# Cross-attention and FFN: the Gate's tokens turned in the attention stage, in 32x32 blocks on VectorE and by plain DMAs, in place of transposing DMAs

## The chip, the cores and the metric

The kernel runs on one core of a Trainium2 chip. The core has five engines, each with an instruction stream of its own: PE (TensorE: matmuls, and transposes as matmuls with an identity), DVE (VectorE), ACT (ScalarE), POOL (GpSimd) and SP (SyncE, which only issues DMAs). 16 DMA engines move data between HBM and SBUF, the on-chip memory of 128 partitions; PE writes PSUM. An engine works through its stream in order: an instruction that waits holds all that stand behind it. The metric is the device time of one execution in microseconds, the median of several runs.

## The reference

```
x:   [16, 512, 512] f32      16 elements of 512 tokens with 512 features
ctx: [16, 120, 512] f32
x1 = x + attention(layernorm(x), ctx)          16 heads of 32, RoPE on queries and keys
t  = act_qdq(layernorm(x1))                    16-bit quantization, one scale for the whole tensor
up   = act_qdq(t @ w_up.T)                     weights quantized to 4 bits in blocks of 32
gate = act_qdq(t @ w_gate.T)                   1536 hidden features
gate = act_qdq(gate * sigmoid16(gate))
out  = x1 + act_qdq(gate * up) @ w_down.T
act_qdq(v): s = max|v| / 32767;  clip(round(v / s)) * s
```

The scale of `act_qdq` is taken over all 16 elements. So no token can be quantized for the FFN until the last element's attention is done, and the normalized tokens must be kept or made again in between.

## The kernel before

**Layout.** Tokens come with tokens on the partitions: an element is four tiles of 128 tokens by 512 features (index q). The FFN's matmuls need them turned: features on the partitions, 4 chunks (index d) of 128 features, by 512 tokens.

**Stages.** Attention (about the first 940 us of the trace), Gate (to about 1495), Up with the sigmoid and the product of gate and up (to about 2050), Down (to the end). In attention and in all three others the order on PE, DVE and ACT is written out by hand (`manual_schedule`), from Gate on POOL's too. What is left to SP, and in attention to POOL, is ordered by the framework's scheduler from its own estimates. The framework also gives the DMAs eight completion semaphores in turn, whatever queue issues them: a DMA is issued only when the one eight places before it has landed.

**Attention.** The loop runs over elements b, and inside it over four rounds g (groups of four heads). In a round PE makes the scores (L338), DVE reduces them to maxima (L344, L349), PE turns the maxima (`tm`, L356), DVE prepares them (L358 to L365), PE subtracts them (L373), ACT takes the exponential (L381), and PE forms values and sums (L389, L394). Between these stand the parts of the other elements: the queries of the next one (L317, L226 to L230), the reciprocals (L405, round 0), divisions (L418, round 1) and outputs (L424, L430, rounds 2 and 3) of the one before (`old`), the normalization of the element two ahead (`new`: statistics L112 on DVE in round 2, `normalize` L303 on POOL, PE's turn `tp_x` L212 in round 3), and the weight preparation for the FFN (`weight`).

The element two behind (`older`) has its x1 = x + attention in `xt`. `end()` (L441) stores x1 to HBM (`x1_d`). `end_normalize(q)` (L446, POOL) makes the normalized tokens `xn`, and `largest(q)` (L454, DVE) reduces them to their largest magnitude in `max_x`; q = 0 in round 0, q = 1 to 3 in round 2. The normalized tokens are then dropped. The last two elements are finished behind the loop (L654 to L679), the last with its normalization on DVE.

**First tokens.** Element 0 alone is turned early: in the last element's four rounds, `first_tokens` (L542) loads its x1 again, normalizes it on POOL, turns it on PE (`transposed`, L207: four PE transposes into a PSUM bank and one ACT copy) and leaves it in two buffers of the pool `ahead` (tag "a", two buffers, each [128, 2, 512] f32). The same two buffers are used by later stages.

**Gate.** `over_all` and `scale_of` (L702, L720) form the scale from `max_x`. L915 quantizes element 0 from the two buffers, `high` and `low` (L758, L761, L768) split it in three pieces of fewer bits, which are the matmuls' operands (`xm`, `xl`, `xh`). PE then works through 96 chunks (element b, two blocks f of 128 hidden features), some 5.4 us each. For the elements after the first, `load(b)` (L901) fetches x1 to `x1t` (one buffer), `normalize` (L920, POOL) normalizes it again, `quantize` (L927) converts it to 16-bit integers on ACT (`xi`) and a transposing DMA (L934, on SP's queue) puts it into `xq` (one buffer). Weights are loaded by `wg.load` (L753), 256 KB each, into 13 buffers for each of three kinds.

Of the kernel before, what the change touches and what calls it, by code (L numbers as in the profile page):

```python
# [9 lines left out]
F32 = mybir.dt.float32  # L10
F32R = mybir.dt.float32r
I32 = mybir.dt.int32
I16 = mybir.dt.int16
# [8 lines left out]
P = 128  # L22
# [31 lines left out]
def tile_xattn_ffn(  # L54
# [42 lines left out]
    xn_d = [dram.tile([P, ND, S], I16, name=f"xn_{b}") for b in range(B)]  # L97

    wg_d, wu_d, wd_d = (dram.tile([P, NF, 3, D], F32, name=f"w{k}_d") for k in "gud")
    x1_d = [dram.tile([NQ, P, D], F32, name=f"x1_{b}") for b in range(B)]  # L100

    g_d = dram.tile([B, P, 2, NF, S // 2], F32, name="g_d")
# [85 lines left out]
    with ExitStack() as at:  # L188
# [95 lines left out]
        class Element:  # L284
# [167 lines left out]
            def largest(self, q):  # L452
                i = self.b * NQ + q
                nc.vector.tensor_reduce(  # L454
                    max_x[:, i : i + 1], self.xn.pop(q), AX.X, ALU.max,
                    apply_absolute_value=True,
                )

        keys = {0: Keys(0)}
        wv_sb = load_weight(wv, "wv_sb", p1)  # L460
# [76 lines left out]
            )  # L537


        first = [ahead.tile([P, 2, D], F32, tag="a", name=f"first_{i}") for i in range(2)]  # L540

        def first_tokens(q):  # L542
            t = first[q // 2][:, q % 2, :]
            nc.sync.dma_start(t, x1_d[0][q])
            nc.gpsimd.tensor_scalar(
                t, t, ln_mv[:, 0, q, 0:1], ln_rstd[:, 0, q : q + 1], ALU.subtract, ALU.mult
            )
            transposed(t, P, t.rearrange("p (d t) -> p d t", t=P), f"first_{q}")

        for q in range(NQ):
# [14 lines left out]
        for b in range(B):  # L568
# [8 lines left out]
            for g in range(NG):  # L577
                if g == 0:
                    here.attend()
                    if older:  # L580
                        for q in range(3):
                            older.end_normalize(q)
                here.scores(g, keys[b // BC].kT)

                rest = []
                if g < 3:
                    if nxt:
                        rest.append(nxt.query((0, 2, 3)[g]))
# [12 lines left out]

                if weight and g == 2:
                    weight.load()
                if weight and g == 3:
                    weight.quantize()
                if older and g == 0:
                    older.largest(0)
                    older.end_normalize(3)
                if older and g == 2:
                    for q in range(1, NQ):  # L610
                        older.largest(q)
                if new and g == 2:
                    for q in range(NQ):
                        new.stats(q)
                    for q in range(3):
                        new.normalize(q)
                if b == B - 1:
                    first_tokens(g)

                if g == 0:  # L620
                    if old:
                        old.reciprocals()
                    if nxt:
                        nxt.query(1)()
                if g == 1 and old:
                    for i in range(2):
                        old.divide(i)
                if g < 2 and kvs:
                    kvs.go_on(2)
                if g == 1 and old:  # L630
                    for i in range(2, NG):
                        old.divide(i)
                if g == 2 and old:
                    for q in range(2):
                        old.output(q)()
                if g == 3:
                    if new:
                        new.turn(0)
                        new.normalize(3)
                    if old:  # L640
                        old.output(3)()
                        old.end()
                        old.inverse()
                    if new:
                        new.turn(1)
                    if weight:
                        rest = weight.turn(0)
                    if new:
                        new.turn(2)
                        new.turn(3)  # L650
                    if weight:
                        rest()
# [11 lines left out]
        for q in range(NQ):  # L664
            old.end_normalize(q)
            old.largest(q)
        for g in range(NG):
            last.divide(g, halves[1])
        for q in range(NQ):
# [4 lines left out]
            if q > 0:  # L674
                last.end_normalize(q - 1, nc.vector)
                last.largest(q - 1)
        last.end()
        last.end_normalize(NQ - 1, nc.vector)
        last.largest(NQ - 1)  # L679

        idle = bank("idle_0")
        for _ in range(18):
# [131 lines left out]
    with ExitStack() as gu:  # L814
# [84 lines left out]
        xs = {0: Tokens(0, "g")}  # L899

        def load(b):  # L901
            xs[b] = Tokens(b, "g")
            xs[b].x1 = wp.tile([P, NQ, D], F32, tag="x1t", name=f"x1t_{b}", bufs=1)
            nc.sync.dma_start(xs[b].x1, x1_d[b].rearrange("q p d -> p q d"))

        wg.load(range(4), (0,))
        wg.load(range(4), (1, 2))
        wg.load(range(4, 8))
        load(1)
        s_x, r_x = scale_of(over_all([max_x], "x"), 1.0, "x")  # L910
        s_xw = small.tile([P, 1], F32, name="s_xw")

        xs[0].room()
        for i, t in enumerate(first):
            nc.vector.tensor_scalar(  # L915
                xs[0].q[:, 2 * i : 2 * i + 2], t.rearrange("p q (d t) -> p q d t", t=P),
                r_x, None, ALU.mult,
            )

        def normalize(b, qs):  # L920
            for q in qs:
                nc.gpsimd.tensor_scalar(
                    xs[b].x1[:, q, :], xs[b].x1[:, q, :],
                    ln_mv[:, b, q, 0:1], ln_rstd[:, b, q : q + 1], ALU.subtract, ALU.mult,
                )

        def quantize(b):  # L927

            xi = wp.tile([P, NQ * D], I16, tag="xi", name=f"xi_{b}")
            nc.scalar.activation(  # L930
                xi, xs[b].x1.rearrange("p q d -> p (q d)"), AF.Copy, scale=r_x
            )
            xs[b].room()
            nc.sync.dma_start_transpose(xs[b].q.rearrange("p q d t -> p (q d) t"), xi)  # L934


        def up_weight(o):
# [21 lines left out]
        for d in range(ND):  # L959
            xs[0].high(d, nc.vector if d < 2 else nc.gpsimd)  # L960
            xs[0].low(d)
        normalize(1, range(NQ))
        xs[0].keep()
        nc.vector.tensor_scalar(s_xw, s_x, WHOLE, None, ALU.mult)

# [44 lines left out]
        for b in range(B):  # L1010
            for f in range(N2):
# [14 lines left out]
                def after():  # L1026
# [20 lines left out]
                    if b + 2 < B:  # L1047
                        if b > 0 and f == 0:
                            load(b + 2)
                        if f in ((2, 3) if b else (3, 4)):  # L1050
                            normalize(b + 2, (0, 1) if f == (2 if b else 3) else (2, 3))
                    if b == B - 1:
                        wu.load((0,) if f == 0 else (2 * f - 1, 2 * f))

# [479 lines left out]
```

## Time and profile before

| | |
|---|---|
| runs | 2598.81, 2604.08, 2605.47 us; median 2604.08 |
| profiled execution | 2608.83 us, of it span 2607.0 us; granted TensorE clock 0.986 |
| busy in the span | PE 2512.7 us (96%), DVE 2083.6 (80%), POOL 1576.6 (60%), ACT 1155.9 (44%) |
| DMA | 500.49 MB in 268146 packets, 192 GB/s |
| PE in Gate | a matmul of 128x128 by 512 tokens each 389 ns |
| `normalize` (L922) | 60 on POOL, 2137 ns each |
| quantization (L930) | 15 on ACT, 1990 ns each |
| transposing DMAs (L934) | 15 on SP's queue, 5.0 us from issue to landing |
| `largest` (L454) | 64 on DVE, 675 ns each |

The span runs from the first to the last instruction of the profiled execution. A row such as `527.13 1.86 DVE L454 TENSOR_REDUCE max_x<-xn 128x1 f32<-128x512 f32 x3` in the timeline reads: start and length in us, engine, line, operation, what is written from what, shapes, and how many like ones are merged; in brackets, where there are any, the idle time of the engine ahead of it and what ended it. SPq and ACTq are DMA issues by those engines. DMA share is the mean busy share of the 16 DMA engines.

### The profile page before, as it was taken

The page shows a single profiled execution, that of the slowest core. Times are in us where ns is not written, and L with a number is a line of the kernel's source. Part 1 is how long each engine was busy: PE and PEld are TensorE (multiplying, and loading weights), DVE is VectorE, ACT ScalarE, POOL GpSimd, SP SyncE. Part 2 cuts the span into 40 slices and gives each one's busy share as a digit, 9 for nine tenths or more (in the row PEclk, how much of TensorE's full clock was granted, in tenths as well). Part 3 has the DMA queues.
Part 4 walks back from the last instruction along what each step waited for, and adds up shares of the span by engine and source line. Part 5 has one row for each costly group of instructions (what it writes and reads, how often), then busy time and mean ns, then how long its engine had stood idle before and what let it go on. Part 6 is the DMA issues. An engine that isn't in the chain of part 4 may idle for free. (4 is left out here: it accounts for less than half of the span.)

```text
span 2607.0 us, 30411 instructions
## 1 busy us (share of the span) xinstructions
PE 2512.7 (96%) x10732; PEld 1690.9 (65%) x10732; DVE 2083.6 (80%) x2836; ACT 1155.9 (44%) x1311; POOL 1576.6 (60%) x1011
## 2 busy tenths in 40 slices
PE   8899999999999889999999999999999699999999
PEld 4334344333433268888878888888887478788887
DVE  4668886887888667786887589999998688888886
ACT  1222232222222225545445378888877344444442
POOL 3466665655675165545555057777766477777775
PEclk9899999999999989999999999999999799999999
DMA  4011121111120086767766789999889777777774
GB/s 161 20 65 49 49 93 59 57 59 49 49 77 33 22 277 214 250 202 244 226 217 217 238 300 332 322 344 330 296 290 322 295 280 253 248 248 248 251 249 145
DMA packets 268146, 500.49 MB, mean 192 GB/s; under 512 B 47440, under 2 KB 66000, under 8 KB 267984
## 3 DMA queue, kind: packets, MB, share of 16 engines
q1 hardware_dynamic: 267296, 496.90, 55.6%
q8 instruction: 85, 1.39, 0.2%
q10 hardware_dynamic: 528, 1.05, 0.1%
q14 instruction: 77, 0.63, 0.1%
q0 software_dynamic: 160, 0.52, 0.1%
HBM read 263.00 MB, written 227.54 MB: 188 GB/s over the span
## 5 line engine op out<-in xcount | busy, mean ns | idle before, releaser
L758 POOL TENSOR_SCALAR oh_d<-oq_d 128x512 fp32r<-128x512 int16 x190 | 398.0, 2117 | 160.8 <-DVE oq_d L1320 134.1
L1106 POOL TENSOR_TENSOR po<-gt,t_wu 128x1024 f32<-128x1024 f32 x96 | 231.7, 2413 | 208.2 <-DVE gt L1083 149.6
L317 PE MATMUL qp<-xnT,wq_sb 128*128 128x512 f32 x512 | 239.2, 610 | 2.5 <-ACT cT L213 2.5
L398 ACT COPY ao<-pv 128x512 f32<-128x512 f32 x64 | 37.5, 586 | 452.2 <-PE pv L389 452.2
L424 PE MATMUL op<-wo_sb,ao 128*128 128x512 f32 x512 | 233.2, 604 | 0.2 <-DVE ao L418 0.2
L1337 PE MATMUL dn_d<-wd,om_d 128*128 128x512 f32 x768 | 196.7, 406 | 22.7 <-DVE om_d L768 13.4
L782 PE MATMUL mm_wg<-xl_g,wg 128*128 128x512 f32 x768 | 205.4, 389 | 0.0
L782 PE MATMUL mm_wg<-xh_g,wg 128*128 128x512 f32 x768 | 205.4, 389 | 0.0
L868 PE MATMUL mm_wg<-xm_g,wg 128*128 128x512 f32 x768 | 195.7, 396 | 6.8 <-DVE xm_g L768 3.6
L1320 DVE SCALAR_TENSOR_TENSOR oq_d<-pq_d,r_o,uq_d 128x1024 int16<-128x1024 int16 x96 | 127.3, 1326 | 90.1 <-ACT uq_d L1273 90.1
L229 POOL TENSOR_TENSOR rt_q<-rt_q,sin_q 128x512 f32<-128x512 f32 x64 | 81.3, 1271 | 185.0 <-DVE rt_q L226 185.0
L1337 PEld LDWEIGHTS dn_d<-wd,om_d 128*128 128x128 f32 x768 | 145.9, 194 | 68.3 <-DVE om_d L768 31.0
L758 POOL TENSOR_SCALAR xh_g<-xq_g 128x512 fp32r<-128x512 int16 x60 | 117.5, 1982 | 116.6 <-DMA xq_g<-xi 111.2
L1337 PE MATMUL dn_d<-wd,ol_d 128*128 128x512 f32 x768 | 184.6, 389 | 1.0 <-ACT dn_d L1349 1.0
L1337 PE MATMUL dn_d<-wd,oh_d 128*128 128x512 f32 x768 | 184.5, 389 | 0.0
L782 PE MATMUL mm_wu<-xl_u,wu 128*128 128x512 f32 x672 | 180.5, 390 | 1.3 <-ACT mm_wu L874 1.3
L317 PEld LDWEIGHTS qp<-xnT,wq_sb 128*128 128x128 f32 x512 | 93.3, 192 | 134.9 <-issue 111.0
L782 PE MATMUL mm_wu<-xh_u,wu 128*128 128x512 f32 x672 | 179.7, 389 | 0.0
L344 DVE TRANSPOSE_TENSOR_REDUCE mt<-st 128x32 f32<-128x1024 f32 x128 | 151.6, 1222 | 30.2 <-PE st L338 30.1
L891 DVE TENSOR_REDUCE max_g<-t_wg 128x1 f32<-128x1024 f32 x96 | 116.5, 1214 | 72.4 <-ACT t_wg L886 72.4
L424 PEld LDWEIGHTS op<-wo_sb,ao 128*128 128x128 f32 x512 | 94.5, 192 | 116.9 <-issue 104.6
L868 PEld LDWEIGHTS mm_wg<-xm_g,wg 128*128 128x128 f32 x768 | 142.9, 190 | 38.9 <-DVE xm_g L768 6.3
(266 smaller groups left out, 5682.7 us busy)
## 6 DMA issues: line engine op xcount, KB each, us to landing
g_d<-t_wg SPq DMA_DIRECT2D x96, 512.0 KB, 3.7
gt<-g_d SPq DMA_DIRECT2D x96, 512.0 KB, 5.4
u_d<-t_wu SPq DMA_DIRECT2D x90, 512.0 KB, 5.8
p_d<-gt SPq DMA_DIRECT2D x90, 512.0 KB, 5.1
p<-p_d SPq DMA_DIRECT2D x90, 512.0 KB, 6.0
u<-u_d SPq DMA_DIRECT2D x90, 512.0 KB, 5.3
xt<-in_x_dram SPq DMA_DIRECT2D x16, 1024.0 KB, 5.3
x_d<-x SPq DMA_DIRECT2D x32, 512.0 KB, 5.0
```

What stands on the lines that cost most here:

```text
L229: nc.gpsimd.tensor_tensor(v(t), v(t), sin, ALU.mult)
L317: nc.tensor.matmul(ps, lhsT=wq_sb[:, d, ts(g, P)], rhs=self.xnT[:, d, :], start=(d == 0), stop=(d == ND - 1),)
L344: nc.vector.tensor_reduce(self.mt[:, 2 * i : 2 * i + 2, 0, :], self.st[i].rearrange("p h (c j) -> p h c j", j=DK), AX.X, ALU.max, apply_tr ...
L398: nc.scalar.copy(self.ao[:, g, :], pv)
L424: nc.tensor.matmul(ps, lhsT=self.ao[:, g, ts(q, P)], rhs=wo_sb[:, g, :], start=(g == 0), stop=(g == NG - 1),)
L758: engine.tensor_scalar(as_runs(p.hi, q), q, TO_256, TO_256, ALU.add, ALU.subtract)
L782: nc.tensor.matmul(ps[:, j, :], lhsT=lhs(j, i)[k], rhs=rhs(j, i)[k], start=(k == 0 and i == 0), stop=(k != 1 and i == n - 1), skip_group_c ...
L868: nc.tensor.matmul(self.ps[:, j, :], lhsT=lhs(j, d), rhs=self.x.p[d].mix, start=(d == 0), stop=(d == ND - 1), skip_group_check=True,)
L891: nc.vector.tensor_reduce(maxes[:, i : i + 1], self.t, AX.XYZ, ALU.max, **how)
L1106: nc.gpsimd.tensor_tensor(flat(g.po), flat(g.tile), flat(c.t), ALU.mult)
L1320: nc.vector.scalar_tensor_tensor(out=oq.rearrange("p f t -> p (f t)"), in0=pq, scalar=r_o, in1=uq, op0=ALU.mult, op1=ALU.mult,)
L1337: nc.tensor.matmul(self.ps[j], lhsT=self.p[f // 2].all()[k][:, f % 2, ts(j, P)], rhs=wd.made[f][k], start=(k == 0 and f == 0), stop=(k != ...
```

## The change

The normalized tokens that `largest` has reduced are no longer dropped. A new method `turn_out(q)` follows each `largest(q)`: DVE turns the tile in blocks of 32x32 into a buffer of the pool `ahead` (two tiles of an element share a buffer, so every element uses both buffers), and four DMAs, one for each 32 partitions, put the blocks to their places in a new HBM tensor `xt_d[b]`, which holds the element turned. Each DMA moves 64 KB, in runs of 32 f32 numbers on both sides. SP issues them; for the last two elements ACT does.

In Gate `load(b)` reads `xt_d[b]`, 8 KB in one piece for each partition, for element 0 too. `normalize`, `first_tokens` and the transposing DMA are gone. `quantize` converts on ACT from `x1t` straight into `xq`, in four pieces; element 0's conversion is done on DVE in four pieces in place of two. `load(0)` stands behind the first twelve `wg` loads in the source and `load(1)` behind element 0's conversion. x1 itself is still stored, since Down adds it.

```diff
+    xt_d = [dram.tile([P, ND, S], F32, name=f"xt_{b}") for b in range(B)]
...
             def largest(self, q):
                 i = self.b * NQ + q
                 nc.vector.tensor_reduce(
-                    max_x[:, i : i + 1], self.xn.pop(q), AX.X, ALU.max,
-                    apply_absolute_value=True,
-                )
+                    max_x[:, i : i + 1], self.xn[q], AX.X, ALU.max, apply_absolute_value=True
+                )
+
+            def turn_out(self, q):
+
+                if q % 2 == 0:
+                    self.out = ahead.tile([P, 2, D], F32, tag="a", name=f"turned_{self.b}_{q}")
+                t = self.out[:, q % 2, :]
+                nc.vector.transpose(t, self.xn.pop(q))
+                to = xt_d[self.b].rearrange(
+                    "(j c) d (q a r) -> a q c d j r", j=P // 32, q=NQ, a=P // 32
+                )
+                for a in range(P // 32):
+                    (nc.scalar if self.b > B - 3 else nc.sync).dma_start(
+                        to[a, q], t[ts(a, 32), :].rearrange("c (d j r) -> c d j r", d=ND, r=32)
+                    )
...
-        first = [ahead.tile([P, 2, D], F32, tag="a", name=f"first_{i}") for i in range(2)]
-
-        def first_tokens(q):
...
                 if older and g == 0:
                     older.largest(0)
+                    older.turn_out(0)
                     older.end_normalize(3)
                 if older and g == 2:
                     for q in range(1, NQ):
                         older.largest(q)
+                        older.turn_out(q)
...
-                if b == B - 1:
-                    first_tokens(g)
...
             old.largest(q)
+            old.turn_out(q)
...
                 last.largest(q - 1)
+                last.turn_out(q - 1)
         last.end()
         last.end_normalize(NQ - 1, nc.vector)
         last.largest(NQ - 1)
+        last.turn_out(NQ - 1)
...
         def load(b):
-            xs[b] = Tokens(b, "g")
-            xs[b].x1 = wp.tile([P, NQ, D], F32, tag="x1t", name=f"x1t_{b}", bufs=1)
-            nc.sync.dma_start(xs[b].x1, x1_d[b].rearrange("q p d -> p q d"))
+            xs.setdefault(b, Tokens(b, "g"))
+            xs[b].x1 = wp.tile([P, ND, S], F32, tag="x1t", name=f"x1t_{b}", bufs=1)
+            nc.sync.dma_start(xs[b].x1, xt_d[b])
 
         wg.load(range(4), (0,))
         wg.load(range(4), (1, 2))
+        load(0)
         wg.load(range(4, 8))
-        load(1)
         s_x, r_x = scale_of(over_all([max_x], "x"), 1.0, "x")
...
-        for i, t in enumerate(first):
+        for d in range(ND):
             nc.vector.tensor_scalar(
-                xs[0].q[:, 2 * i : 2 * i + 2], t.rearrange("p q (d t) -> p q d t", t=P),
+                xs[0].q[:, :, d, :], xs[0].x1[:, d, :].rearrange("p (q t) -> p q t", t=P),
                 r_x, None, ALU.mult,
             )
-
-        def normalize(b, qs):
...
+        load(1)
 
         def quantize(b):
-
-            xi = wp.tile([P, NQ * D], I16, tag="xi", name=f"xi_{b}")
-            nc.scalar.activation(
-                xi, xs[b].x1.rearrange("p q d -> p (q d)"), AF.Copy, scale=r_x
-            )
             xs[b].room()
-            nc.sync.dma_start_transpose(xs[b].q.rearrange("p q d t -> p (q d) t"), xi)
+            for d in range(ND):
+                nc.scalar.activation(
+                    xs[b].q[:, :, d, :], xs[b].x1[:, d, :].rearrange("p (q t) -> p q t", t=P),
+                    AF.Copy, scale=r_x,
+                )
...
-        normalize(1, range(NQ))
...
-                        if f in ((2, 3) if b else (3, 4)):
-                            normalize(b + 2, (0, 1) if f == (2 if b else 3) else (2, 3))
```

More of the change, by code (lines that the diff above doesn't have):

```diff
@@ L537, in gate_weight @@
             )
-        first = [ahead.tile([P, 2, D], F32, tag="a", name=f"first_{i}") for i in range(2)]
-        def first_tokens(q):
[L543 to L546, printed above, removed]
-            )
-            transposed(t, P, t.rearrange("p (d t) -> p d t", t=P), f"first_{q}")
         for q in range(NQ):
@@ L913, in tile_xattn_ffn, with quantize @@
         xs[0].room()
-        for i, t in enumerate(first):
+        for d in range(ND):
             nc.vector.tensor_scalar(
-                xs[0].q[:, 2 * i : 2 * i + 2], t.rearrange("p q (d t) -> p q d t", t=P),
+                xs[0].q[:, :, d, :], xs[0].x1[:, d, :].rearrange("p (q t) -> p q t", t=P),
                 r_x, None, ALU.mult,
             )
-        def normalize(b, qs):
[L921 to L924, printed above, removed]
-                )
-        def quantize(b):
-            xi = wp.tile([P, NQ * D], I16, tag="xi", name=f"xi_{b}")
-            nc.scalar.activation(
-                xi, xs[b].x1.rearrange("p q d -> p (q d)"), AF.Copy, scale=r_x
-            )
-            xs[b].room()
-            nc.sync.dma_start_transpose(xs[b].q.rearrange("p q d t -> p (q d) t"), xi)
+        load(1)
+        def quantize(b):
+            xs[b].room()
+            for d in range(ND):
+                nc.scalar.activation(
+                    xs[b].q[:, :, d, :], xs[b].x1[:, d, :].rearrange("p (q t) -> p q t", t=P),
+                    AF.Copy, scale=r_x,
+                )
         def up_weight(o):
```

## The prediction

> **What bounds the kernel now.** The 40 slices of the page come first, then busy time by stage, then the timeline of one element. The run is one core: span 2607.0 us, 2608.83 us around it, 4.75 us above the median of 2604.08. I work in differences and add them to the median.
>
> ```profile
> 155.00:870.00 715.00, 694.03 (x2867) 279.64 (x2865) 572.46 (x1033) 183.35 (x249) 447.18 (x408) 1.00 0.17 58
> 915.00:943.00 28.00, 24.41 (x65) 13.00 (x65) 19.86 (x41) 0.41 (x1) 14.49 (x28) 0.87 1.02 376
> 943.00:975.00 32.00, 29.02 (x127) 23.61 (x127) 16.31 (x23) 12.00 (x13) 20.12 (x10) 0.92 0.62 196
> 975.00:1490.00 515.00, 511.17 (x2295) 421.57 (x2294) 394.09 (x446) 249.24 (x274) 257.29 (x136) 1.00 0.70 224
> ```
>
> (Columns: stretch and length, then busy us of PE, PEld, DVE, ACT, POOL; granted clock, DMA share, GB/s.) PE sets the pace: idle 21 us of 715 in attention, 3.8 of 515 in Gate. So Gate has almost nothing to give. The end of attention (915 to 943) is the one stretch where the 16 DMA engines are full. DVE has 20% free in attention, but an average doesn't say where. Element 8, round 2:
>
> ```profile
> 527.13 1.86 DVE L454 TENSOR_REDUCE max_x<-xn 128x1 f32<-128x512 f32 x3
> 528.91 0.68 DVE L112 BATCH_NORM_STATS2 st_a<-xt 128x6 f32<-128x512 f32 x1
> 532.11 0.66 DVE L430 TENSOR_TENSOR xt<-op,xt 128x512 f32<-128x512 f32 x1
> 533.83 0.69 DVE L430 TENSOR_TENSOR xt<-op,xt 128x512 f32<-128x512 f32 x1
> 535.38 2.35 DVE L344 TRANSPOSE_TENSOR_REDUCE mt<-st 128x32 f32<-128x1024 f32 x2
> 537.76 0.20 DVE L349 COPY mt<-mt 128x64 f32<-128x64 f32 x1
> 538.33 0.27 PE L356 MATMUL tm<-ident,mt 128*128 128x128 f32 x1
> ```
>
> DVE is without a pause from the three `largest` to L349; PE's `tm` starts 0.37 us after L349 ends. Where PE waits in earnest that distance is 0.06, so round 2 has 0.31 us of slack, and 0.1 more ahead of the second L430. In round 0 the same element has none:
>
> ```profile
> 506.00 0.67 DVE L454 TENSOR_REDUCE max_x<-xn 128x1 f32<-128x512 f32 x1
> 506.59 3.35 DVE L405 RECIPROCAL rc<-sm 128x512 f32<-128x512 f32 x1
> 511.08 2.37 DVE L344 TRANSPOSE_TENSOR_REDUCE mt<-st 128x32 f32<-128x1024 f32 x2
> 514.29 0.33 PE L356 MATMUL tm<-ident,mt 128*128 128x128 f32 x1 [0.37 <-DVE mt L349]
> ```
>
> PE already waits there. At the end of attention:
>
> ```profile
> 933.82 0.37 SPq L904 DMA_DIRECT2D x1t<-x  x1
> 935.97 0.39 ACTq L441 DMA_DIRECT2D x<-xt  x1
> 939.76 0.69 DVE L454 TENSOR_REDUCE max_x<-xn 128x1 f32<-128x512 f32 x1
> 943.02 1.42 DVE L915 TENSOR_SCALAR xq_g<-first,inv_x 128x1024 int16<-128x1024 f32 x2
> 946.74 0.70 PE L868 MATMUL mm_wg<-xm_g,wg 128*128 128x512 f32 x2
> ```
>
> The last maximum, then the scale 2.6 us later, then L915 at once, since element 0's tokens are already turned in SBUF; PE starts Gate 3.7 us after L915 begins.
>
> **The DVE transposes.** 64 are added, 128x512 f32, and the trace shows none. Nearest row: L454, the same tile read by the same engine, 0.675 us. From below L446 on DVE, 0.52 (128x512, f32 both sides); from above, a whole L344, 1.22, for half its elements. I take 0.67, because L344, which turns, takes 1.22 us for 1024 elements a lane, as long as the plain reduction L891 (1.21).
>
> The Trainium skill's "VectorE: DVE Perf Modes", section "The three transpose paths", gives 311 ns for 128x128 bf16; four of these would be an estimate of 1.24 us a transpose, and by it the sum would be that of rival 2 below; the trace speaks for the shorter one, and no run yet shows the operation.
>
> Round 2 gets three (2.01 us) ahead of the statistics and L430. Of elements 2 to 13 each loses 2.01 - 0.31 - 0.10 = 1.60: 12 x 1.60 = 19.2 us. Elements 14 and 15 have no new statistics there and DVE waits for PE's `output` (4.37 us in element 15), which hides them. Round 0 gets one, ahead of L405: by the distance from L349 to `tm` in round 1, elements 3, 4, 8, 12, 13, 14, 15 have no slack (7 x 0.67 = 4.7), 7 and 11 have 0.6 (0.15 together), 2, 5, 6, 9 and 10 have 0.7 or more. Sum 4.85. PE works in order and is the bound elsewhere, so none of it is recovered. What else is late by 2 us, POOL's `normalize` of the element after next, is needed by PE's `tp_x` 2 us after it is ready (543.95 against 546.02) and PE is late itself: nothing. Together +24.0; at 0.52, 13.8 + 3.6 = 17; at 1.22, 39 + 11 = 50.
>
> **The placing DMAs in the loop.** Per element 16 on SP's queue (each 64 KB in 512 runs of 128 B), 131072 runs in all. An issue takes 0.32 to 0.5 us by the DMA rows of 256 KB; 16 x 0.4 = 6.4 us of an element's 50, and SP sits idle. Queued behind them are the x load (L290, wanted two elements later), the weight load and the x1 store; the weight stores that ACT's `rh` waits for come before them. Price of a run: by the trace's packet records 11 ns at 112 B, 25 at 512 B, 84 at 2 KB. Scattered stores of 128 B are not among them; the bounds are 11 and 84, and I take 25, the row of the scattered 512 B stores to `wd_d`, which land in 2.3 us. A copy is then 512/16 x 25 ns = 0.8 us of full engines, an element's 16 are 13 us, at a DMA share of 0.17 now: hidden. At 84 they would be 43 us of 50, just hidden.
>
> The same page section warns that a plain DMA that does the transpose by its strides is 19 times slower than the transposing one. The transposing rows here land in 5.0 us, so by the rule an element's copy is an estimated 95 us, the loop runs at 95 instead of about 50 us an element, and 14 x 45 = 630 us are lost. I weigh it low: DVE has turned the blocks, and the runs are 32 whole elements.
>
> **The stage boundary.** This is the second loss; its times are those of the run before, to which the loop's shift is added. In the changed program as built, `load(0)` stands on SP behind all 36 loads of `wg` that fit (before, 32 came ahead of `load(1)`, and nothing waited for that), and a DMA is issued only when the eighth before it, on any queue, has landed (a load issued at 916.85 landed at 922.24, its eighth successor left at 922.25). The 32 copies of elements 14 and 15, issued by ACT, now stand between the `wg` loads, one after each two, and the lane of `load(0)` was last used by the eighth copy of element 15. The first copy can't leave before DVE turned it, 920.9; 43 more positions follow up to the last copy of element 14. Eight in flight with 5.4 us to landing (the `wg` rows in a full queue) or 4 (my estimate where the small copies thin it out): 5.4 rounds, 22 to 29 us, so that lands near 946 to 953. Then the second turned buffer is free for element 15's third transpose (two buffers; DVE is held, and behind it stand the last maximum, the scale and L915), and the eight copies of element 15's first half need one more round of about 2.5 us (256 KB stores land in 2.0 to 2.4). `load(0)` leaves about 949 to 955 and lands 5.3 to 7.8 us later (the 1 MB rows of `xt` and `x1t`), beside the 1 MB store of x1_15. Queued behind it on SP are the first raw up and down weights and `load(1)`, wanted 15 us later; behind ACT's copies only L874, which waits for PE anyway. L915's successor starts at 954 to 963 instead of 943.0: +11 to +20, I take +15. The four conversions in place of two, and the transposes in the tail (1.6 us ahead of L418, 0.7 ahead of the scale), hide in this wait; were it gone, they would cost 2.5 and the extra loads nothing, so the lower bound is +2.5. At 50 ns a run, 24 copies ahead of `load(0)` are 38 us of full engines and the 36 loads 24 us (0.68 each): 911 + 62 + 5 = 979, +36; at 84 it is +60.
>
> **What is taken away.** 16 PE transposes of `first` (0.66 a group): rounds 2 and 3 of element 15 are on PE's path, -1.3. POOL's 60 normalizations (128 us), 15 transposing DMAs: Gate's PE waits for neither (POOL waits 111 us for the DMAs, PE idles 3.8 in all), 0. ACT converts in four pieces, 4 x 0.62 against 1.99, 0.5 more, hidden in 44% use. It now waits itself for the xq buffer: the last reader ended at 1008.8, ACT started at 1017.3: nothing.
>
> Sum: 19.2 + 4.85 + 15 - 1.3 = +37.7. Median 2604.1 + 37.7 = 2642.
>
> **The rivals.** (1) Transposes hidden, boundary clean: DVE's 20% absorbs them and `load(0)` is in time, which decides when the placing copies land in about 1 us and the scheduler's order does not bind. Then +2.5 - 1.3, less at most 3.8 of Gate's idle: 2601 to 2606, not slower. For it: the average use. Against it: L344 has no idle time before it in 12 elements. (2) Transposes at 1.22: 50 + 15 - 1.3, 2668. For it: no row shows one; against it: L344's rate. (3) Copies dear: 128 B runs at 50 ns; 24 + 36 - 1.3, 2663; at 84, 2687. For it: no row is so small and so scattered; against it: price falls with size in every row.
>
> **How the numbers follow.** Forecast 0.64; rival 1 0.10; rival 2 0.12; rival 3 0.14. The forecast's own range is 17 to 24 plus 11 to 20: 2630 to 2650. Opening to rivals 2 and 3 and half way to rival 1: 2612 to 2675. 0.3% (7.8 us) is what can be told from no change. Faster by that is beyond rival 1 except for its lower tail, 0.03; same 0.08; slower 0.89.
>
> **What would show it.** L344 of round 3 starting 1.6 us later against PE's `output`, with `tm` waiting for DVE in elements 2 to 13; the element's period up from 50 by 2; transposes at 0.67; the DMA share of the loop at 0.3 to 0.4; SP issuing `x1t` near 950 + 24 and PE's first L868 some 15 us later against the last `output`; Gate as long as before. It is wrong if attention keeps its length, if the transposes last over 1 us, or if DVE waits for DMAs in the loop.

## The result and the profile after

| | before | changed |
|---|---|---|
| median of 4 runs each, on one chip | 2603.6 us | 2630.8 us (2628.0 to 2636.1) |
| profiled span | 2607.0 us | 2628.5 us |

The ratio is 1.011, 95% interval 1.0089 to 1.0131: 27 us slower. Cut at the same instructions in both traces (`tm` is the `tm` matmul of element 15, round 3):

| stretch | before | changed | difference |
|---|---|---|---|
| start to `tm` of element 15 | 903.3 | 919.0 | +15.7 |
| `tm` to the first Gate matmul | 43.45 | 58.62 | +15.2 |
| Gate, to the first Up matmul | 541.1 | 534.9 | -6.1 |
| Up, to the first Down matmul | 557.7 | 555.1 | -2.6 |
| Down, to the last instruction | 561.5 | 560.8 | -0.7 |

The windows by stage of the changed kernel (columns as in the prediction) show where to look: PE idles 40 us of 730 in attention (21 of 715 before), and 0 of 515 in Gate (3.8 before).

```profile
155.00:885.00 730.00, 690.37 (x2848) 278.09 (x2844) 597.80 (x1079) 183.06 (x248) 433.90 (x402) 1.00 0.28 74
930.00:958.00 28.00, 23.55 (x58) 11.78 (x58) 19.77 (x37) 0.40 (x1) 13.72 (x23) 0.88 1.08 350
958.00:990.00 32.00, 17.33 (x65) 13.21 (x66) 12.66 (x28) 2.02 (x2) 5.48 (x8) 0.73 0.71 205
990.00:1505.00 515.00, 515.00 (x2319) 426.45 (x2318) 390.15 (x452) 267.08 (x326) 151.53 (x83) 1.00 0.59 210
```

**Round 2 of an element.** The timeline of element 8:

```profile
533.50 0.70 DVE L465 STREAM_TRANSPOSE turned<-xn 128x512 f32<-128x512 f32 x1
...
535.88 0.69 DVE L465 STREAM_TRANSPOSE turned<-xn 128x512 f32<-128x512 f32 x1
...
541.19 0.66 DVE L432 TENSOR_TENSOR xt<-op,xt 128x512 f32<-128x512 f32 x1
...
542.71 2.35 DVE L346 TRANSPOSE_TENSOR_REDUCE mt<-st 128x32 f32<-128x1024 f32 x2
545.09 0.24 DVE L351 COPY mt<-mt 128x64 f32<-128x64 f32 x1
545.38 0.33 PE L358 MATMUL tm<-ident,mt 128*128 128x128 f32 x1 [1.13 <-DVE mt L351]
```

PE now waits for DVE at `tm`. From `tm` of round 2 to `tm` of round 3 elements 2 to 13 each take 1.27 to 1.29 us more, and from there to the next element's first `tm` another 0.48 to 0.51 (the exponentials' matmuls wait 0.60 for `nm`, 0.16 before): 1.78 an element, 21.3 us in all. Elements 14 and 15 lose nothing here.

The second part has another cause than the first: the short conversion behind `tm`, on the way to `nm`, is longer. In the timeline of element 8 before, and then of the changed kernel:

```profile
536.95 2.07 POOL L303 TENSOR_SCALAR xn<-xt,mv,rstd 128x512 f32<-128x512 f32 x1
538.97 0.19 DVE L362 CAST mh<-mx 128x32 fp32r<-128x32 f32 x1
```

```profile
544.51 2.08 POOL L305 TENSOR_SCALAR xn<-xt,mv,rstd 128x512 f32<-128x512 f32 x1
546.07 0.56 DVE L364 CAST mh<-mx 128x32 fp32r<-128x32 f32 x1
```

It now falls under one of POOL's `normalize` instructions and ends 0.04 us after it; before, that instruction was over 0.05 us after the conversion began.

**Round 0.** The transpose ahead of the reciprocal moved `tm` of round 1 by only 0.05 us in elements 4, 8, 12 and 13. The timeline of the kernel before, and then of the changed one, says why:

```profile
512.92 1.26 POOL L229 TENSOR_TENSOR rt_q<-rt_q,sin_q 128x512 f32<-128x512 f32 x1
513.48 0.75 DVE L349 COPY mt<-mt 128x64 f32<-128x64 f32 x1
```

```profile
518.67 1.27 POOL L231 TENSOR_TENSOR rt_q<-rt_q,sin_q 128x512 f32<-128x512 f32 x1
519.81 0.20 DVE L351 COPY mt<-mt 128x64 f32<-128x64 f32 x1
```

The same small copy lasts 0.75 us before and 0.20 after; both times it ends 0.05 to 0.07 us after POOL's instruction. Its length held a wait of 0.55 us, and the transpose filled it. In element 3 the same copy took 1.03 us before and 0.20 after, and `tm` of round 1 comes 0.59 us earlier than before.

**The stage boundary.** The timeline at the end of attention:

```profile
926.42 30.34 SPq L760 DMA_DIRECT2D wg<-wg_d  x36
965.95 0.32 SPq L911 DMA_DIRECT2D x1t<-xt  x1
```

```profile
935.60 32.80 ACTq L470 DMA_DIRECT2D xt<-turned  x28
968.44 0.64 ACTq L443 DMA_DIRECT2D x<-xt  x1
```

```profile
961.45 0.71 DVE L465 STREAM_TRANSPOSE turned<-xn 128x512 f32<-128x512 f32 x1 [2.71 <-DMA xt<-turned]
...
966.25 0.17 DVE L734 RECIPROCAL inv_x<-scale_x 128x1 f32<-128x1 f32 x1
971.72 1.67 DVE L922 TENSOR_SCALAR xq_g<-x1t,inv_x 128x512 int16<-128x512 f32 x4 [5.30 <-DMA x1t<-xt]
975.21 0.86 DVE L765 TENSOR_SCALAR xh_g<-xq_g 128x512 fp32r<-128x512 int16 x1 [1.81 <-DMA x<-xt]
```

Three waits stand in a row, and all lead to ACT's queue: a transpose waits for a buffer that a copy still reads, the scale is ready 7.7 us later than before (counted from `tm`), L922 waits 5.3 more for element 0's load, and the first high half 1.8 for the store of x1_15, which ACT issues behind 28 copies. That the load stands behind the copies too, through the completion lanes, is in SP's waits from 925 to 970 us (total, times, longest):

```profile
SPq L911 <- DMA xt<-turned: 9.1, 1, 9.1
```

What is left of attention's +15.7: elements 5 and 9, where PE waits for the context's loads (`ct`, 3.2 us in all, 0.2 before), +2.2 and +1.0 (in element 5 the granted clock was also 0.50 from 347.4 to 350.8 us); element 15 without the first tokens, -1.6; element 2, -3.5; and element 0, -3.3, which the change doesn't touch (the granted clock was 0.90, 0.76 and 0.66 in the three stretches of 10 us from 70 us on before, and 1.00, 0.90 and 0.76 after).

Element 2's gain belongs, by the trace, to the first tokens. POOL ran their four normalizations there, from 166 to 176 us, and not in the last element, where the source has them. In the kernel before VectorE's short instructions were long beside them, and PE waited:

```profile
173.75 2.09 POOL L545 TENSOR_SCALAR first<-first,ln_mv,ln_rstd 128x512 f32<-128x512 f32 x1
175.35 0.53 DVE L362 CAST mh<-mx 128x32 fp32r<-128x32 f32 x1
178.43 0.51 PE L373 MATMUL st<-nm,ones 32*128 32x512 f32 x4 [1.59 <-DVE nm L365]
```

The changed kernel has no wait there. The wait is 1.6 of the 3.5 us; the rest is a granted clock of 0.50 from 180.4 to 183.8 us before and full after, which may be chance. All 13 profiles without the first tokens gain 3.5 us at this place; no run takes the first tokens away by themselves. Element 0's 3.3 us are in the profile before and not shown for the medians: this may be one reason why the profile's +21.5 is less than the medians' +27.

### The profile page after: what moved, and what is told of

Read it like the earlier page. It is cut to its first block, busy times and chain, and to the rows that moved or that the text cites. A ratio compares the mean times of both kernels' runs of the same rounds, so it can differ in the third digit from the quotient of the medians.

```text
span 2628.5 us, 30827 instructions
## 1 busy us (share of the span) xinstructions
PE 2507.9 (95%) x10716; PEld 1688.2 (64%) x10716; DVE 2106.6 (80%) x2902; ACT 1165.7 (44%) x1352; POOL 1447.3 (55%) x947
```

## The experiments

All ratios are to the kernel before, run on the same chip. Line numbers of an experiment are its own.

**1. The transposes spread over the rounds.**

```diff
+                if g == 0 and 3 <= b < B - 1:
+                    el[b - 3].turn_out(3)
...
+                if g >= 2 and older and new:
+                    older.turn_out(g - 1)
...
                         older.largest(q)
-                        older.turn_out(q)
```

> The changed kernel with its transposes of elements 0 to 12 moved on VectorE: the first stays where it is, the second and third go between scores and maxima of rounds 2 and 3 (where VectorE waits 1.09 and 0.68 us for PE's tm), the fourth between those of the next element's round 0 (1.13 us); nothing is left out. Theory, the loop's loss is VectorE's full round 2 (3 x 0.70 - 0.31 = 1.79 us in each of 12 elements, 21.4 together): tm of round 3 keeps its 0.37 us of slack again, the element's period falls by 1.7 to 1.8, attention by 20 to 22 and the time to about 2610 (2605 to 2616). Rival, the copies or a VectorE with no room anywhere are what lengthens the loop: tm moves elsewhere or stays late, and more than 10 us of the 21 remain (over 2620).

Measured: 2631.5 us, ratio 1.0102 (1.0077 to 1.0127): nothing gained. `tm` of round 3 is on time (0.00 to 0.01 us late in place of 1.28), but the next stretch loses 1.38 to 1.48 (1.90 behind element 13) in place of 0.50, and round 0 another 1.07 in elements 4, 8, 12 and 13. PE's timeline in this run:

```profile
554.65 0.66 PE L214 MATMUL tp_x<-ident,xn 128*128 128x128 f32 x4 [1.24 <-POOL xn L305]
```

A transpose that comes later holds its normalized tile longer. The three `xn` buffers are shared with the next element's `normalize`, so POOL starts late and PE waits for it. Half the theory stands (round 2 is cured), and the loss took a new place. Elements 5 and 9 also lose 4.7 and 3.1 us in round 1. Whether VectorE has room was not yet answered.

**2. Spread without holding the buffers.**

```diff
+                if g in (1, 2) and older and new:
+                    older.turn_out(g)
...
                         older.largest(q)
-                        older.turn_out(q)
+                        if q == 3 or not new:
+                            older.turn_out(q)
```

> The changed kernel with two transposes moved on VectorE that no longer hold a normalized tile (xn, three buffers, shared with the next element's normalize) beyond round 2: the first stays, the second goes between scores and maxima of round 1 (0.42 us of wait there), the third between those of round 2 (1.09), the fourth stays in round 2's full block. Nothing is left out. Theory, the first spreading failed only because its transposes held the xn buffers (PE waits 1.24 us a round 3 for POOL's xn) and doubled round 0: now round 2 carries 0.70 - 0.31 = 0.39 and round 1 at most 0.28, so an element loses 0.4 to 0.7 in place of 1.79, attention falls by 13 to 17 us and the time to 2614 to 2618. Rival, VectorE has no room at any place and the loss follows the work wherever it goes: 1.5 to 1.8 an element remain, over 2625.

Measured: 2627.6 us, ratio 1.0092 (1.006 to 1.0125): above the expected 2614 to 2618. Round 2 to 3 loses 0.07 to 0.26 in place of 1.28, as expected; round 3 keeps its 0.49, with the conversion behind `tm` 0.55 us long under POOL's instruction as in the changed kernel. But elements 5 and 9 lose 5.5 and 5.3 us each in round 1, where the changed kernel lost 2.2 and 1.0. PE's timeline in element 5:

```profile
345.74 1.96 PE L214 MATMUL tp_c<-ident,ct 120*128 120x120 f32 x8 [4.15 <-DMA ct<-in_ctx_dram]
```

The second transpose's copies now stand on SP's queue ahead of the context's loads, which PE needs at once. The copies in the loop are not free after all.

**3. Twice the copies.** Each placing copy of elements 0 to 13 is repeated into a tensor that nobody reads.

> The changed kernel in which every placing copy of elements 0 to 13 is made twice, the second time into a tensor that nobody reads: 224 copies more on SP's queue. Nothing is left out. Theory, the copies in the loop are hidden (SP is idle, engines' DMA share 0.2 to 0.3): round 3 of elements 2 to 13 loses the same 1.28 + 0.50 us, attention keeps its length within 3 us. Rival, the loop's loss is the copies' (SP's issue of 0.63 us each, or their traffic): twice the copies give twice the loss, attention 15 to 21 us longer.

Measured: 2663.5 us (one run). Round 3 loses the same 1.28 + 0.50, so the copies aren't what delays `tm` there. But attention grew by 20 us over the changed kernel, as much as the rival said, though in other places, so "hidden" fell as a general statement: PE waits 10.1 us for `ct` (3.2 in the changed kernel, 0.2 before), and in seven elements `tm` of round 1 is later than in the changed kernel. In elements 4, 8, 12 and 13 it is 1.3 us: VectorE waits 0.43 us for POOL there, and its copy then meets POOL's next instruction (1.02 us long). In elements 3, 7 and 11 it is 2.5 us with a copy of 0.20 us; VectorE waits longer for POOL there (3.34 and 2.06 us in element 7). Why VectorE waits for POOL, and not in the changed kernel, is not settled. The boundary took 13 us more. SP issues 32 copies an element in this run, at 0.63 us each 20 of 51 us, and what stands behind them comes later.

**4. Round 0's transpose twice.** One line more, into the half of the buffer that is overwritten next:

```diff
                     older.turn_out(0)
+                    nc.vector.transpose(older.out[:, 1, :], older.xn0)
```

> The changed kernel with round 0's transpose made twice in elements 2 to 15 (the second into the half that the next transpose overwrites). Nothing is left out. Theory, the first cost nothing because the copy L351 of round 1 waits for the end of a POOL instruction anyway (0.75 us long before, 0.20 after): a second one puts that copy 0.7 later, beyond that end and under POOL's next instruction (1.27 us), so tm of round 1 is later by about 1.3 us in elements 4, 8, 12, 13, more than the transpose itself. Rival, plain order on VectorE: 0.6 to 0.7 there. Second rival, there is other slack: nothing.

Measured: 2634.4 us (one run). `tm` of round 1 is 1.34 to 1.35 us later than before in elements 4, 8, 12 and 13 (0.05 with one transpose): more than the 0.70 that was added, as the theory said, and 0.41 of it comes back in round 2. The timeline of element 8:

```profile
518.52 1.26 POOL L232 TENSOR_TENSOR qT<-ra_q,rt_q 128x512 f32<-128x512 f32 x1
```

```profile
518.95 0.89 DVE L351 COPY mt<-mt 128x64 f32<-128x64 f32 x1
```

The copy again ends with POOL's instruction, this time the next one. Its end goes in steps of POOL's instructions, and both the free first transpose and the dear second one follow from that; so does the 0.49 us of round 3, where the changed kernel's L364 is held in the same way. This agrees with the Trainium skill, "SBUF — State Buffer", section "Who interferes with whom": a VectorE copy in a two-port mode and GpSimd lock the same pair of SBUF ports for a whole instruction, and whoever comes second waits.

**5. and 6. The boundary's buffers, and then its load.** In run 5 elements 14 and 15 are turned into two free `xt` buffers; in run 6 element 0's tokens are also loaded early.

```diff
+                if self.b > B - 3:
+                    if q == 0:
+                        self.out = p2.tile([P, NQ, D], F32, tag="xt", name=f"turned_{self.b}", bufs=4)
+                    t = self.out[:, q, :]
```

```diff
+        first = []
+        for i in range(2):
+            first.append(ahead.tile([P, 2, S], F32, tag="a", name=f"first_{i}"))
+            nc.sync.dma_start(first[i], xt_d[0][:, 2 * i : 2 * i + 2, :])
...
-        load(0)
```

> The changed kernel with elements 14 and 15 turned into two free 8 KB buffers of their own (those of xt), so that no transpose of theirs waits for a placing copy to leave its buffer; the load of element 0 stays where it is. Nothing is left out. Theory A, VectorE is held by the two turned buffers (2.97 + 2.71 us of waits ahead of the last maxima, and the scale is ready at 966.4): scale and L922 come 4 to 7 us earlier against the last output. Theory B, the place of element 0's load decides (behind 36 weight loads and, through the lanes, behind the copies; issued at 965.95, landed at 971.63): the scale comes earlier, but the load and with it L922 move by less than 2 us, and PE's first Gate matmul stays 13 to 15 us later than in the kernel before, counted from attention's tm of element 15, round 3.

> As the run with own buffers for elements 14 and 15, and element 0's turned tokens are loaded before the end of attention into the two buffers that have come free, so that Gate's first scaling waits for no load there. Nothing is left out. Theory, the boundary's 15 us are the load and the held VectorE together: PE's first Gate matmul comes at most 3 us later than in the kernel before, counted from tm of element 15, round 3 (four conversions for two, and the last transposes, remain); the time falls by 10 to 15 us, to 2616 to 2621. Rival, the 32 copies beside the 36 weight loads fill the DMA engines, and the first weights or the last statistics are late: more than 8 of the 15 us remain, over 2623.

Measured: counted from `tm`, run 5 (2635.2 us, one run) has the scale at 42.2 us (47.4 in the changed kernel, 39.7 before), but L922 at 55.9 (52.7): theory B, the load decides, and it even came later. Run 6 has L922 at 42.3, as hoped, and yet PE's first Gate matmul at 63.9 us, 20 us later than before; 2639.8 us, ratio 1.0134 (1.0107 to 1.0162). The timeline of run 6:

```profile
940.44 33.94 ACTq L475 DMA_DIRECT2D xt<-turned  x28
974.42 0.64 ACTq L443 DMA_DIRECT2D x<-xt  x1
```

```profile
985.25 0.43 DVE L774 TENSOR_SCALAR xh_g<-xq_g 128x512 fp32r<-128x512 int16 x1 [17.97 <-DMA x<-xt]
```

Gate's first pieces lie where attention's `xt` lay, and wait for the store of x1_15, which stands on ACT's queue behind 28 copies as before. Each cured wait uncovers the next one; what doesn't move is the end of the 28 copies. Both theories of run 6 missed this.

**7. Both edits together**, run 1 with run 6.

> Both edits in one: the transposes spread over the rounds, own buffers for elements 14 and 15, and element 0's tokens loaded early. Nothing is left out. Theory, the losses add: 2630.8 less 21 less 10 to 15 is 2595 to 2600, below the kernel before by 4 to 9 us, because Gate has gained 6 us (PE's idle time 6.8 to 0.8) and the first tokens' PE transposes 1.6. Rival, Gate's gain was an accident of the two profiles: then the two losses gone give 2602 to 2606, the time of before.

Measured: 2636.9 us, ratio 1.0123 (1.0104 to 1.0142), with both defects above. Gate took 535.5 us. In all 13 profiles without its transposing DMAs, or with two of them, it took 534.4 to 536.6 us, so its gain is no accident of one profile after; before there is one profile alone, with 541.1.

**8. No copies at the boundary.** Elements 14 and 15 go the way of the kernel before (rows, POOL, transposing DMA inside Gate), and element 0 is loaded early as in run 6.

```diff
             def turn_out(self, q):
+                if self.b > B - 3:
+                    return
...
+            if b > B - 3:
+                nc.sync.dma_start(xs[b].x1, x1_d[b].rearrange("q p d -> p q d"))
```

> The changed kernel with elements 14 and 15 on the way of the kernel before (loaded by rows, normalized by POOL and turned by a transposing DMA inside Gate; no transpose and no placing copy at the end of attention), and element 0's turned tokens loaded before the end of attention. Nothing is left out. Theory, the boundary's 15 us are the 32 copies of ACT's queue (0.58 to 0.65 us an issue, 20 us in all, with the store of x1_15 behind 28 of them) and the load behind them: PE's first Gate matmul comes at most 3 us later than in the kernel before, counted from tm of element 15, round 3, and the time falls by 11 to 14 us to 2617 to 2620. Rival, Gate's start is late for another reason (new order of SP's loads, tokens in xt): 6 us or more remain, over 2624.

Measured: 2617.7 us, ratio 1.0052 (1.0035 to 1.0069). The first Gate matmul is at 43.06 us after `tm` (43.45 before, 58.62 changed). The boundary's 15 us are the copies of the last two elements on ACT's queue and the load behind them. This run leaves out these elements' transposes too, a smaller part: run 6, which keeps them, had L922 2.6 us later than L915 before. The timeline of this run shows x1_15's store free of them and L937 (L922 in the changed kernel) right after the scale:

```profile
948.32 0.39 ACTq L443 DMA_DIRECT2D x<-xt  x1
```

```profile
954.97 0.16 DVE L740 RECIPROCAL inv_x<-scale_x 128x1 f32<-128x1 f32 x1
955.17 1.67 DVE L937 TENSOR_SCALAR xq_g<-first,inv_x 128x512 int16<-128x512 f32 x4
956.76 0.42 DVE L771 TENSOR_SCALAR xh_g<-xq_g 128x512 fp32r<-128x512 int16 x1
```

**9. Runs 2 and 8 together.**

> The spread of the run before last (second transpose in round 1, third in round 2's gap, fourth in the block) and the last two elements on the old way, with element 0's tokens loaded early. Nothing is left out. Theory, both losses go: 2630.8 - 15 - 12 = 2604 (2600 to 2608), the time of the kernel before, because the loop's 0.4 to 0.7 an element (5 to 8 us) and the boundary's 2 eat up what Gate gained (6) and the first tokens (1.6). Rival, if either cause is wrong: over 2612.

Measured: 2614.0 us against 2606.3, ratio 1.0031 (1.0016 to 1.0047), 8 us above and over the rival's bound. The two causes hold (the boundary is at 44.7 us, rounds 2 and 3 of an element lose 0.6 to 0.8 together), but a third was left in: elements 5 and 9 lose 5.0 us each to `ct`, as in run 2.

**10. and 11. What shortened Gate.** Run 10 puts POOL's normalizations back on a spare tile; run 11 makes ACT's conversion one instruction.

```diff
+                                nc.gpsimd.tensor_scalar(
+                                    spare, xs[b + 2].x1[:, q, :], ln_mv[:, b + 2, q, 0:1],
+                                    ln_rstd[:, b + 2, q : q + 1], ALU.subtract, ALU.mult,
+                                )
```

```diff
-            for d in range(ND):
-                nc.scalar.activation(
-                    xs[b].q[:, :, d, :], xs[b].x1[:, d, :].rearrange("p (q t) -> p q t", t=P),
-                    AF.Copy, scale=r_x,
-                )
+            nc.scalar.activation(
+                xs[b].q.rearrange("p q d t -> p d q t"),
+                xs[b].x1.rearrange("p d (q t) -> p d q t", t=P), AF.Copy, scale=r_x,
+            )
```

> The changed kernel with POOL's normalizations of Gate put back at their places for elements 2 to 15, on a spare tile that nobody reads (four of 2.07 us an element). Nothing is left out. Theory, Gate (first Gate matmul to first Up matmul) became 6.1 us shorter because POOL has less to do: its high halves and so VectorE's low halves and xm come earlier, and VectorE's copies meet fewer POOL instructions; then most of the 3.8 us of PE's waits in Gate's middle are back: 537.5 to 541 in place of 534.9. Rival, ACT's four short conversions in place of one long did it: Gate stays at 534.9 to 535.5.

> The changed kernel with ACT's conversion of elements 1 to 15 in one instruction over the whole tile in place of four. Nothing is left out. Theory (POOL's work is what shortened Gate): Gate stays at 534.9 to 536. Rival (a long ACT instruction holds up the copies t_wg, on which PE waited 2.6 us before): Gate goes to 537 to 539, with PE's waits for t_wg back.

Measured: Gate took 534.4 us in both (534.9 changed, 541.1 before); 2629.6 and 2630.0 us, one run each. Run 10 did the work that it added:

```profile
L1052 POOL TENSOR_SCALAR spare<-x1t,ln_mv,ln_rstd 128x512 f32<-128x512 f32 x56 | 123.2, 2200 | 15.1 <-DMA x1t<-xt 11.3
```

(Groups of lines: busy us and mean ns, then idle time ahead.) Neither POOL's load nor the length of ACT's instruction, each by itself, shortened Gate; my theory and its rival are both wrong. What is left to suspect first is the transposing DMA itself. Before, POOL waited for it: in one element ACT's conversion ended at 1294.2 and POOL's high halves began at 1301.9, and PE's 0.98 us wait for `xm` came at 1322.4. That this is the cause is argued, not shown; no run isolates it.

**12. A version that beats both.** Run 9 with the fourth maximum moved into round 3's gap, read from the turned tile, and the context's loads issued ahead of the copies.

```diff
+                if g == 3 and older and new:
+                    older.largest(3, older.out[:, 1, :])
...
+                    if g == 0 and b % BC == 1:
+                        for i in range(2, BC):
+                            kvs.fetch(i)
```

> The two edits of the last combined run, with two more: the fourth maximum moves from round 2's block to between scores and maxima of round 3 (where VectorE waits 0.68 us) and reads the turned tile, so that the block carries two maxima and one transpose (1.94 us against 1.86 in the kernel before); and the loads of the context (ct) are put ahead of the placing copies on SP's queue. Nothing is left out. Theory: of the loop's loss the 0.49 us of round 3 in 12 elements and PE's waits for ct in elements 5 and 9 (8.5 us in the spread run) go; attention is as long as in the kernel before less the 1.6 of the first tokens, Gate 5 to 6 us shorter, its start 1.3 later: 3 to 8 us below the kernel before, ratio 0.997 to 0.999. Rival, VectorE has no room for 2.8 us more in 50 us: ratio over 1.001.

Measured: 2595.4 us against 2603.7, ratio 0.9973 (0.9959 to 0.9986). Round 2 to 3 loses 0.01 us at most and round 3 at most 0.17 an element; elements 5 and 9 still 1.0 and 0.9; Gate starts 42.99 us after `tm` and takes 536.4. At `tm` the profile is 2.6 us ahead of the kernel before, with element 2's 3.5 in it, and Gate gives 4.7. Round 2 and 3 of element 8 in its timeline:

```profile
523.76 1.27 DVE L460 TENSOR_REDUCE max_x<-xn 128x1 f32<-128x512 f32 x2
524.95 0.70 DVE L471 STREAM_TRANSPOSE turned<-xn 128x512 f32<-128x512 f32 x1
...
532.00 2.35 DVE L350 TRANSPOSE_TENSOR_REDUCE mt<-st 128x32 f32<-128x1024 f32 x2
534.39 0.20 DVE L355 COPY mt<-mt 128x64 f32<-128x64 f32 x1
534.50 0.68 DVE L460 TENSOR_REDUCE max_x<-turned 128x1 f32<-128x512 f32 x1
```

Two maxima and one transpose stand where three maxima stood, and the moved maximum fills the time in which VectorE waited for PE's `tm`. All four transposes are there, 2.8 us an element: VectorE had the room, but not where the change put three of them.

## Why the prediction was right, and where it wasn't

The direction and the time's place in the range held: 2630.8 in 2612 to 2675, at the lower part (2642 forecast), +27 for +37.7. The two large terms came out nearly as forecast, in part by luck; gains that the sum put at nothing did the rest. By its steps:

- **Round 2, 19.2 predicted, 21.3 measured.** Right in place, mechanism and elements, but the near match is partly luck. What the prediction reckoned, `tm` waiting for a fuller VectorE, cost 1.28 an element, 15.4 us, and not 1.60: a transpose took 0.70 (0.67 taken), but instructions in a row overlap by some 0.1 us, so three of them moved the statistics by 1.81. Of that 0.26 was taken up on the way to L344, most of it by the slack ahead of the second L430, and the copy added 0.04, so the stretch from the first maximum to L349's end grew from 10.83 to 12.42 us in element 8; less the 0.31 of slack at `tm` that is 1.28. The other 0.49 an element, 5.9 us, is L364 under POOL's `normalize`. The prediction has no such term: it saw that `normalize` would be late, asked only who needs its result, and wrote "nothing".
- **Round 0, 4.85 predicted, -0.4 measured.** Elements 4, 8, 12 and 13 lose 0.05 each, 5 loses 0.12 and 3 gains 0.59. This step failed: "Round 0 gets one, ahead of L405: by the distance from L349 to `tm` in round 1, elements 3, 4, 8, 12, 13, 14, 15 have no slack". The distance was read from L349's end; the slack was inside L349, 0.75 us long in place of 0.20 (1.03 in element 3, 0.94 in 14). The prediction looked at neither the copy's length in that round nor POOL's lines.
- **The copies in the loop, hidden.** Right in the main: run 3 leaves round 3 as it was, a run of 128 B took 13 ns by the packet records (25 taken; the lower bound of 11 rests on five packets of 112 B in the trace before, and its 30720 packets of 256 B, at a median of 18 ns, were left aside), and the DMA share is 0.28 (0.3 to 0.4 said). Wrong in one place: the list of what is queued behind them left out the context's loads, which cost 3.2 us in elements 5 and 9. And an issue took 0.63 us, not 0.32 to 0.5.
- **The boundary, +15 predicted, +15.2 measured.** The load was issued 46.9 us after `tm`; 45.7 to 51.7 was predicted (949 to 955, less 903.3). So close a match is partly luck, since only part of the chain was told: the load delays L922 by 13.0 in all, and of the other 2.2, 1.8 are the wait for the store of x1_15 behind the copies, which the prediction dismissed ("behind ACT's copies only L874"). Its lower bound of +2.5 for a clean boundary fits run 6 as far as L922 (42.3 against 39.7); run 8, which has no transposes there either, starts Gate 0.4 us earlier than before and doesn't test it.
- **First tokens, -1.3:** -1.6 measured in element 15, and 3.5 more in element 2, where POOL's normalizations of them held VectorE (1.6) and the clock was lower besides (the rest). The prediction counted PE's transposes of them in the last element and not POOL's work.
- **Gate as long as before:** wrong by 6.1 us, the transposing DMAs' waits being the suspected and not the shown cause. Of that 3.8 were named as its idle time and called worth nothing ("Gate's PE waits for neither"), and 2.2 stood at its start.
- **Rivals.** Transposes at 1.22 us: 0.70 measured. Dear copies: 13 ns a run. Everything hidden and a clean boundary: the changed kernel isn't there; run 12 is, with another order.

With the measured terms the sum is 21.3 - 0.4 + 3.2 + 15.2 - 1.6 - 3.5 - 6.1 = +28.1; the medians say +27. Element 0's -3.3 and the -2.6 and -0.7 of Up and Down are left out of it: Up took 552.9 to 557.8 us in the 14 profiles, so no part of it is put down to the change.

The rules of the skill that were weighed ("VectorE: DVE Perf Modes", section "The three transpose paths") both spoke for a larger loss. The page has 311 ns for 128x128 bf16, and the estimate of four times that, 1.24 us, for a 128x512 f32 tile compares with 0.70 us measured. Its 19 times is for a copy that turns by its strides when the innermost stride at the destination is large; the copies here, of whole 128 B runs, are not of that kind and landed in 2.2 us.

## What to carry to other kernels

Work added to an engine with idle time costs what the fullest stretch between two hand-overs lacks, not what the average leaves; put it in the gap just behind such a hand-over, and count which buffers it holds until then. A cheap store that nobody waits for still stands in an issue queue: name every load and store behind it, at the ends of a stage above all, and follow the chain past the first wait, since curing one only uncovers the next. Look at the length of short instructions too: one that takes three times its usual time holds a wait that no idle column shows, and which engine it waits for can be read from whose instruction ends just before it. A sum that fits is no proof of its terms: here 3 x 0.70 - 0.31 = 1.79, as the expectation of run 1 has it, is within 0.01 of the 1.78 us that an element lost, and yet two different waits make these up.

## What the runs showed of the hardware

- A VectorE copy of 64 numbers a lane takes 0.20 us, or until POOL's running instruction ends: 0.75, 0.89 and 1.02 us were seen, so 0.70 us of added work cost 0.05 us once and 1.3 us the second time. The conversion of 32 numbers a lane (0.19 us) was held in the same way under POOL's `normalize`, to 0.56.
- A DMA with 512 runs of 128 B costs its queue mostly 0.57 to 0.66 us an issue (median 0.63 on SP), against 0.32 for the plain 256 KB loads, and 28 of them held ACT's queue for 33 us between `wg` loads that share their completion lanes.
- A 128x512 f32 transpose in 32x32 blocks takes 0.69 to 0.71 us on VectorE, about as long as a plain pass over the tile (0.67).
